# Between the two steps: the order of list sums, logits, moments and keys

## The chip, the cores and the metric

The kernel runs on one core of one Trainium2 chip. The metric is device time in microseconds (us), the median of several executions. A core has five engines with instruction queues of their own: TensorE (PE in the profile, its weight loads PEld), VectorE (DVE), ScalarE (ACT), GpSimd (POOL) and SyncE (SP, which here only issues DMAs). Line numbers (L819) are those of the kernel before.

## The reference

The input is a table of 3327 nodes with 256 features and a sparse weighted adjacency matrix. The table is normalised (layer norm, ReLU) and run through two steps. In each step a list part (`R @ Xf`, over each node's few neighbours) and an attention part (`A @ Xa`, over all nodes) are formed; in the attention, every row keeps only its largest probabilities until they make up 0.9 of the mass.

```python
R = S + jnp.eye(N)
R = R / R.sum(-1, keepdims=True)
for n in range(STEPS):                       # 2 steps
    q = Xa @ W1.T @ W2.T
    k = Xa @ W3.T
    probs = softmax(q @ k.T)
    A = probs * top_p_mask(probs, 0.9)
    A = A / A.sum(-1, keepdims=True)
    Xf = R @ Xf
    Xa = A @ Xa
    Z = Z + Xf @ U1[n].T + Xa @ U2[n].T
return x + layernorm(X + Z) * ln_g + ln_b
```

What matters for the change: keys `k` of step 1 come from `Xa` of step 0, for all nodes. A full row of step-1 logits can't be made before the last tile of step 0 has been summed and its keys are there.

## The kernel before

The nodes are cut into NT = 26 tiles of 128 rows (the last has 127). For each step a loop runs i from -1 to 27, and works on several tiles at once, each at another stage: `measured(i + 1)` guesses a threshold on ACT (passes over a whole row of 3328 elements, `ja`), `settle(i)` finds the exact one on DVE (`w`, `cand`, `bb`, `e`), the class `Sums` transposes the kept weights (`turn`, tiles `pt` and `eT`) and multiplies them with the node table (`sum`, tile `pa`), `spread` forms the list sums of a tile (`diffuse`, tile `pr`) and in step 0 writes the result to `vx` in DRAM, and `weights` makes a tile's logits in four chunks (`pl` on PE, then an exponential into `e` on ACT). In step 0, `first_end(t)` takes a summed tile, transposes it (`xa` to `xT`), multiplies it with the weights of both steps (`pz`: the second half goes to `xw`, the first to `sv` and to DRAM), and calls `prep`, which makes the tile's step-1 keys and queries (`pk` to `after` and `both`).

The order is written out by hand. One turn of the loop has seven slots; a string for each slot names generators by letters, and each letter advances its generator by one `yield`. `PLAN[0]` is the string list of step 0, `PLAN[1]` that of step 1, `OPEN` and `LAST` replace it in the first and last turns of step 1. The letters that matter: `s` list sums, `e` `first_end`, `w` the next logits chunk, `q` a tile's query projection, `m` and `n` `measured`, `d` and `c` `settle`, `g` gathers, `l` `laws` (the statistics of all tiles of step 1). A dependency from each instruction to the next of the same engine, added at the end of the kernel, keeps PE, ACT and DVE in the order of the text from the first turn on, and POOL from the start of step 1 on. SP's DMAs are not held to the text.

Names and lines around the border between the steps, in the order of the text:

- The last two turns of step 0 are i = 26 and i = 27 (NT and NT + 1). Both follow `PLAN[0]`. `spread(0, 24)` (L905, L1079, L1080) runs in slots 0 and 1 of turn 26, `spread(0, 25)` in slots 0 and 1 of turn 27.
- `begun` holds the `weights` generators of step-1 tiles 0, 1 and 2. Three of the four chunks of each are run in turns 24, 25 and 26; the fourth needs the keys of tile 25.
- At the end of turn 26 stand `moments(1, gsum)` (L504 to L510: DVE, PE, DVE) and three `project` calls (L522 on PE, L529 on ACT, L535 on DVE, L538 to L542 on POOL), which give tiles 0 to 2 the statistics that `measured` needs.
- In turn 27 `first_end(25)` makes `pz` (L918), has ACT copy it (L919, L921), and then makes the last keys (L482, L490, L491).
- Step 1 begins with the fourth chunk of tile 0 (`run(begun[0])`, L605, L607), then `prove(0)`, 12 or so small DVE operations (L771 to L788). Then comes turn -1 with `OPEN[-1]`: eight groups of `laws` (PE L554, DVE L557 to L560) on the letter `l`; `measured` of tile 0 on `m` (ACT L617 to L622, passes L630; DVE L681, L682; ACT L683 to L685; pass L630; DVE L695 on; ACT L698 to L701, L708); the fourth chunks of tiles 1 and 2 on two `w` in slot 2; five indirect gathers from `vx` (POOL L897) in slot 3, ahead of POOL's L686 to L688 of slot 4.
- Turn 0 of step 1 settles tile 0 (DVE L725, L730, ...) and measures tile 1. It has four letters `w`, which find nothing to do in the kernel before.

PSUM tiles rotate: `pt` (also used by `pk`, `pq` and others) has two buffers, `pl` two, `pr` (also `pz`) one, `pa` one.

Of the kernel before, what the change touches and what calls it, by code (L numbers as in the profile page):

```python
# [9 lines left out]
F32 = mybir.dt.float32  # L10
# [8 lines left out]
P = 128  # L19
N = 3327  # L20
D = 256
DA = 64
NT = (N + P - 1) // P
# [321 lines left out]
def guess_graph_layer(ctx, tc, x, adj, w1t, w2t, w3t, u1t, u2t, ln_g, ln_b, out, flag):  # L345
# [17 lines left out]
    rows_of = lambda t: min(P, N - t * P)  # L363
# [114 lines left out]
    def prep(xT, t):  # L478
        j, h = divmod(t, 2)
        pk = ps_t.tile([P, 4, P], F32, tag="pt", name="pk")  # L480
        for c in range(ND):
            PE.matmul(pk[:, 0, :], wk[:, c, h * DA : h * DA + P], xT[:, c, :], start=c == 0, stop=c == ND - 1)  # L482
        if t in COUNTED:
            for c in range(ND):
                PE.matmul(pk[:, 1, :DA], xT[:, c, :], wk[:, c, :DA], start=c == 0, stop=c == ND - 1)
        kp = (low, high)[h]
        kr = krs[:, t // 2 % 2, :]
        if t in COUNTED:
            S.copy(kr[:, :DA], pk[:, 1, :DA])
        S.copy(after[kp, j, :], pk[kp, 0, :])  # L490
        S.copy(query_of(t), pk[query_at(t), 0, :])  # L491
        if t not in COUNTED:
            return
        yield
        pg = ps_t.tile([P, 4, P], F32, tag="pt", name="pg")
        PE.matmul(pg[:DA, 0, : DA + 1], kr[:, :DA], kr, start=True, stop=True)
        gt = small.tile([DA, DA + 1], F32, tag="gt", name="gt", bufs=2)
        S.copy(gt, pg[:DA, 0, : DA + 1])
        G.tensor_tensor(gsum, gsum, gt, ALU.add)
# [292 lines left out]
    class Sums:  # L792
# [18 lines left out]
        def sum(self, g):  # L811

            t, k = divmod(g, PARTS)
            if k == 0:
                self.pa = ps_a.tile([P, 2 * D], F32, tag="pa", name="pa")[:, :D]
            eT = self.eT.pop(g)
            for c in range(4 * k, min(4 * k + 4, NT)):
                j = c % HALF * 2 + c // HALF
                PE.matmul(self.pa, eT[:, c - 4 * k, :], self.xa[:, j, :], start=c == 0, stop=c == NT - 1)  # L819
            if k < PARTS - 1:  # L820
                return None
            if self.step:
                return t, (self.pa, self.live.pop((self.step, t))["ra"])
            n = rows_of(t)
            dst = row.tile([P, D], F32, tag="xa", name="xa", bufs=2)
            if n < P:
                V.memset(dst, 0.0)
            S.activation(dst[:n], self.pa[:n], AF.Copy, scale=self.live.pop((self.step, t))["ra"][:n])
            return t, dst

# [82 lines left out]
    def first_end(t):  # L913
        aT = transposed(live.pop(("r", t)))
        yield
        pz = ps_r.tile([P, 2 * D], F32, tag="pr", name="pz")
        for c in range(ND):
            PE.matmul(pz, aT[:, c, :], u2[:, c].rearrange("p n d -> p (n d)"), start=c == 0, stop=c == ND - 1)  # L918
        S.copy(xw[:, t, :], pz[:, D:])  # L919
        sv = row.tile([P, D], F32, tag="sv", name="sv", bufs=2)  # L920
        S.copy(sv, pz[:, :D])  # L921
        G.tensor_tensor(sv, sv, x0[:, t, :], ALU.add)  # L922
        nc.sync.dma_start(sx[t], sv)
        yield
        yield from prep(aT, t)


    def finish(t, y, pa, ra):
# [135 lines left out]
    nc.sync.dma_start(bet, ln_b.to_broadcast([P, D]))  # L1064


    def spread(step, t):
        rr = rrs[:, t : t + 1]
        own = row.tile([P, D + 1], F32, tag="own", name="own", bufs=2)
        nc.sync.dma_start(*((own[:, :D], vx[:, t, :]) if step else (own, bx[:, t, :])))  # L1070
        s1 = row.tile([P, D], F32, tag="s1", name="s1", bufs=4)
        nc.sync.dma_start(s1, (sx if step else ax)[t])
        a, w = acs.pop(t), D + 1 - step
        pr = yield from diffuse(a, xgs.pop(t), own[:, :w], w)
        if step == 0:
            nc.sync.dma_start(cx[t], a.rearrange("p k r -> p (k r)"))
        yield
        if step == 0:
            V.reciprocal(rr, pr[:, D : D + 1])  # L1079
        V.scalar_tensor_tensor(s1, pr[:, :D], rr, s1, ALU.mult, ALU.add)  # L1080
        if step == 0:
            nc.sync.dma_start(vx[:, t, :], s1)
        else:
            live["f", t] = s1

    def refetch(t):
# [11 lines left out]

    LAST = {NT - 1: ("cfss", "cn", "nd", "sss", "fdddddsf", "f", ""), NT: ("c", "", "", "ff", "ff", "fv", "f"),
            NT + 1: ("fv", "f", "", "", "f", "f", "f")}  # L1100
    OPEN = {-1: ("llcmss", "lnms", "lwwnfd", "lcmdsssggggg", "fmgswqdf", "llmdf", "lmwfdm"),
            0: ("cmssggg", "nms", "wwnfd", "cmdsss", "fsmgwqdf", "mdf", "mwd"),
            1: ("cmss", "nms", "wwnfd", "cmdsssggggg", "fsmwqdf", "mgdf", "mwd")}
    OPEN[2] = OPEN[3] = OPEN[1]
# [7 lines left out]
    for step in range(2):  # L1112
        sums = Sums(step, live, xw if step else x0, AHEAD[step])

        for i in range(-1, NT + 2):
            if step == 0 and i == NT - 3:
                begun = [weights(1, t, live, False) for t in range(3)]
            if step == 1 and i == -1:
                ordered.append(len(trace))
            if step == 1 and i == -1:  # L1120
                run(begun[0])
                prove(0)
                for e in es[4:]:
                    G.memset(e[:, N:NP], 0.0)
            work.update(
                n=work["m"],
                c=work["d"],
                d=settle(step, i, live[step, i]) if valid(i) else none,
                m=measured(step, live[step, i + 1]) if valid(i + 1) else none,
                s=spread(step, i - 2 + 2 * step) if valid(i - 2 + 2 * step) else none,  # L1130
                w=later.pop((step, i + 2), none),
                e=first_end(i - 2) if step == 0 and valid(i - 2) else none,
                a=itertools.islice(lister, 9 if i else 3) if step == 0 else none,
                p=packed(i + 1) if step == 0 and i >= 0 and valid(i + 1) else none,
                g=fetching if step else gathered(i) if valid(i) else none,
                b=none, q=none, v=proof() if step and i == NT else work.get("v", none),
                l=laws(range(3, NT)) if step and i == -1 else work["l"] if step and i == 0 else none,
            )
            if i >= 0 and valid(i + 3):
                later[step, i + 3] = weights(step, i + 3, live)  # L1140
                work["q"] = itertools.islice(later[step, i + 3], 2 - step)
            if step == 0 and i >= NT - 2 and i < NT + 1:

                work["w"] = itertools.islice(begun[i - NT + 2], CUT - 1)
            if step == 0 and i >= NT - 3 and i < NT:
                work["q"] = itertools.islice(begun[i - NT + 3], 1)
            if i == -1:
                work["w"] = begun[1] if step == 0 else itertools.chain(begun[1], begun[2])
            if step == 0 and i == 0:
                work["w"] = begun[2]  # L1150
            if step == 0 and i < 1:
                work["b"] = itertools.islice(product, MADE if i else NT)
            for k in range(PARTS):
                g = PARTS * (i - 1) + k - LATE[step]
                summing = valid(g // PARTS)
                if step and valid((g + AHEAD[1]) // PARTS):
                    sums.turn(g + (k == 2), min(i, NT - 1))
                for c in "bb" + ({**OPEN, **LAST}.get(i, PLAN[1]) if step else PLAN[0])[k]:
                    next(work[c], None)
                if summing and not step:  # L1160
                    sums.turn(g, min(i, NT - 1))
                for n in BLOCKS[step].get(k, (0,)) if summing else ():
                    ended = sums.sum(g + n)
                    if ended and step == 0:
                        live["r", ended[0]] = ended[1]
                    elif ended:
                        work["f"] = finish(ended[0], live.pop(("f", ended[0])), *ended[1])
            if step == 1 and i == -1:
                run(work["m"])
            if step == 0 and i == -1:  # L1170
                G.memset(es[2][:, N:NP], 0.0)
            if step and i < 1:
                next(fetching)
            for c in ("lcnwqsepb" if i > -1 else "cnwqsepb") if step else "cmwqsepgb":
                run(work[c])
            if step == 0 and i == NT:
                moments(1, gsum)
                for t in range(3):
                    live[1, t]["ms"] = returned(project(1, t, queries=False))
    run(work["f"])  # L1180

    for engine, since in ((PE.engine, begin), (S.engine, begin), (V.engine, begin), (G.engine, ordered[0])):
# [47 lines left out]
```

## Time and profile before

| | |
|---|---|
| time, median of 3 runs | 1404.44 us (1404.25 to 1408.04) |
| profiled execution, its own time | 1405.77 us |
| its span, first to last instruction | 1404.0 us |
| granted TensorE clock, mean | 0.981 |
| busy share of the span: PE, DVE, ACT, POOL | 91%, 85%, 79%, 57% |
| step 0, last list sum of tile 25 ends on DVE (L1080) | 783.36 us |
| step 1, first full-row scan on DVE (L725), tiles 0, 1, 2 | 806.58, 828.51, 849.98 us |

The profile is of one execution. Its times count from the first instruction. The 1.77 us between its span and its own time lie before and behind the instructions. "Busy" is the time in which an engine executed something; for PE the ends of matmuls are modelled. A bracket behind an instruction gives the idle time of its engine before it and the instruction that ended the wait.

Busy time in 10 us stretches around the border between the steps (us of 10):

| us from start | PE | DVE | ACT | POOL | granted clock |
|---|---|---|---|---|---|
| 740 to 750 | 10.00 | 6.39 | 4.33 | 8.14 | 1.00 |
| 750 to 760 | 10.00 | 1.14 | 3.74 | 2.12 | 1.00 |
| 760 to 770 | 10.00 | 0.17 | 4.13 | 0.10 | 1.00 |
| 770 to 780 | 9.14 | 0.76 | 2.77 | 1.83 | 1.00 |
| 780 to 790 | 8.78 | 6.52 | 4.64 | 4.69 | 1.00 |
| 800 to 810 | 6.48 | 7.62 | 8.89 | 5.44 | 0.67 |
| 820 to 830 | 4.81 | 9.37 | 9.01 | 8.43 | 0.54 |
| 830 to 840 | 8.82 | 9.72 | 8.24 | 8.28 | 1.00 |
| 850 to 860 | 8.86 | 9.89 | 9.02 | 7.79 | 1.00 |

### The profile page before, as it was taken

How to read it: one execution, taken by the hardware profiler on the slowest of the kernel's cores; microseconds unless marked ns; L12 is line 12 of the kernel's file. 1: busy time of each engine (PE TensorE's matmuls, PEld its weight loads, DVE VectorE, ACT ScalarE, POOL GpSimd, SP SyncE). 2: the span in 40 equal slices, each digit the busy share in tenths (PEclk: the TensorE clock that was granted, in tenths of full speed). 3: DMA queues.
4: the chain of work that ended last, by engine and by line, in shares of the span. 5: the costliest groups of instructions: out<-in, count | busy, mean ns of one | idle time of the engine just before them, and what ended most of it. 6: DMA issues, size and time to landing. Idle time of an engine off the chain costs nothing.

```text
span 1404.0 us, 22095 instructions
## 1 busy us (share of the span) xinstructions
PE 1275.7 (91%) x6495; PEld 976.9 (70%) x6495; DVE 1195.0 (85%) x3673; ACT 1105.3 (79%) x2451; POOL 795.3 (57%) x1243
## 2 busy tenths in 40 slices
PE   6897999999999999999999759999999999999985
PEld 5545777777767777777777537777777777777764
DVE  6878898898988979989882489999998999999993
ACT  5467777878877778778773689999998999999941
POOL 6225766666657656666673475655655555565522
PEclk9999999999999999999999879999999999999998
DMA  8884453444444534534422121322312223132200
GB/s 279 269 269 122 118 145 109 128 138 117 128 125 115 143 107 122 146 111 125 126 78 83 51 72 45 90 77 60 91 56 80 67 70 88 50 89 73 63 20 22
DMA packets 91203, 149.77 MB, mean 107 GB/s; under 512 B 15266, under 2 KB 58657, under 8 KB 91073
## 3 DMA queue, kind: packets, MB, share of 16 engines
q1 hardware_dynamic: 73616, 105.37, 23.8%
q0 software_dynamic: 16640, 42.69, 12.3%
q8 instruction: 54, 0.88, 0.3%
q14 instruction: 77, 0.62, 0.1%
q10 hardware_dynamic: 816, 0.20, 0.1%
HBM read 120.93 MB, written 27.28 MB: 106 GB/s over the span
## 4 chain that ended last, share of the span: by engine, by line
PE 43%; DVE 40%; ACT 11%; issue 4%; DMA 1%; POOL 1%; SPq 0%; another core or an unknown queue 0%; DVEq 0%; ACTq 0%; POOLq 0%
PE pa L819 18%; DVE cand L730 8%; DVE w L725 7%; PE pt L805 6%; DVE e L759 5%; PE pr L905 4%; PE pl L597 4%; DVE cand L739 3%; ACT ja L630 3%; DVE bb L737 3%; PE pz L982 3%; PE pz L918 3%; DVE x L759 2%; ACT eT L807 2%; PE pk L1023 1%
## 5 line engine op out<-in xcount | busy, mean ns | idle before, releaser
L819 PE MATMUL pa<-xw,eT 128*128 128x256 f32 x1352 | 323.6, 384 | 27.4 <-DVE s L929 26.2
L630 ACT ACTIVATE ja<-e,g 128x3328 uint8<-128x3328 f32 x106 | 325.7, 3073 | 0.1
L819 PE MATMUL pa<-x,eT 128*128 128x256 f32 x1352 | 325.2, 382 | 0.0
L819 PEld LDWEIGHTS pa<-xw,eT 128*128 128x128 f32 x1352 | 250.7, 190 | 77.9 <-DVE s L929 31.6
L807 ACT COPY eT<-pt 128x512 f32<-128x512 f32 (+1 forms) x364 | 200.6, 559 | 119.8 <-PE pt L805 100.5
L819 PEld LDWEIGHTS pa<-x,eT 128*128 128x128 f32 x1352 | 244.8, 192 | 26.3
L730 DVE MAX8 cand<-w 128x8 f32<-128x168 f32 (+1 forms) x1040 | 251.4, 317 | 0.0
L805 PE MATMUL pt<-ident,e 128*128 128x128 f32 x1144 | 176.1, 276 | 18.2 <-DVE e L756 9.1
L897 POOL DMA_INDIRECT xg<-bx,index x130 | 156.6, 1205 | 45.2 <-issue 31.5
L805 PEld LDWEIGHTS pt<-ident,e 128*128 128x128 f32 x1144 | 140.9, 144 | 57.7 <-issue 29.2
L725 DVE SCALAR_TENSOR_TENSOR w<-e,g 128x3328 f32<-128x3328 f32 x44 | 162.1, 3684 | 0.7
L888 POOL DMA_INDIRECT ac<-in_adj,index x130 | 130.3, 1002 | 44.5 <-issue 29.6
L897 POOL DMA_INDIRECT xg<-vx,index x130 | 129.5, 996 | 38.6 <-issue 38.6
L759 DVE SCALAR_TENSOR_TENSOR e<-e,rec 128x3328 f32<-128x3328 f32 x40 | 147.5, 3688 | 0.6
L905 PE MATMUL pr<-xg,ac 128*128 128x257 f32 (+1 forms) x520 | 140.6, 395 | 6.8 <-DVE s L1080 6.8
L601 ACT ACTIVATE e<-pl 128x832 f32<-128x832 f32 x132 | 113.8, 867 | 17.9 <-PE pl L597 14.4
L905 PEld LDWEIGHTS pr<-xg,ac 128*128 128x128 f32 x520 | 94.0, 194 | 32.1 <-issue 14.2
L737 DVE MAX8 bb<-cand 128x8 f32<-128x160 f32 x286 | 92.6, 324 | 6.4
L597 PE MATMUL pl<-after,qT 64*128 64x416 f32 x416 | 95.5, 553 | 0.0
L597 PE MATMUL pl<-both,qT 64*128 64x416 f32 x416 | 90.4, 538 | 0.8 <-DVE both L1000 0.8
L673 POOL TENSOR_SCALAR g<-g,law 128x1 f32<-128x1 f32 x23 | 46.4, 2017 | 67.4 <-ACT g L672 67.4
L922 POOL TENSOR_TENSOR sv<-sv,x 128x256 f32<-128x256 f32 x26 | 19.8, 763 | 109.9 <-ACT sv L921 109.9
(255 smaller groups left out, 2153.5 us busy)
## 6 DMA issues: line engine op xcount, KB each, us to landing
at<-in_adj SPq DMA_DIRECT2D x102, 256.0 KB
cx<-ac SPq DMA_DIRECT2D x26, 384.0 KB
ac<-cx SPq DMA_DIRECT2D x26, 384.0 KB
wide<-in_adj SPq DMA_DIRECT2D x10, 832.0 KB
e<-in_adj SPq DMA_DIRECT2D x8, 832.0 KB
bx<-e SPq DMA_DIRECT2D x26, 128.5 KB
own<-bx SPq DMA_DIRECT2D x26, 128.5 KB
x<-in_x SPq DMA_DIRECT2D x13, 256.0 KB
```

The costliest lines, as they stand in the source:

```text
L597: PE.matmul(pl[:, a, :wd], qT[p, :], keys_of(step, a).rearrange("p a b -> p (a b)")[:, c : c + wd], start=True, stop=True)
L630: S.activation(ja, e, f, bias=guess, scale=sign, accum_out=total)
L725: V.scalar_tensor_tensor(w, e, col(16), e, ALU.is_lt, ALU.mult, accum_out=d2)
L730: V.max(cand[:, 8 * s : 8 * s + 8], w[:, s * SEG : min(NP, (s + 1) * SEG)])
L737: V.max(b8, cand)
L759: V.scalar_tensor_tensor(e, e, at(1), e, ALU.is_ge, ALU.mult, accum_out=ra)
L805: PE.transpose(pt[:, j, :], e[:, (j0 + j) * P : (j0 + j + 1) * P], ident)
L807: S.copy(eT[:, :w, :], pt[:, :w, :])
L819: PE.matmul(self.pa, eT[:, c - 4 * k, :], self.xa[:, j, :], start=c == 0, stop=c == NT - 1)
L888: G.indirect_dma_start(out=ac[:, k, :], out_offset=None, in_=rows, in_offset=bass.IndirectOffsetOnAxis(ap=index[:, t, k : k + 1], axis=0), ...
L897: G.indirect_dma_start(out=xg[:, k, :w], out_offset=None, in_=rows, in_offset=bass.IndirectOffsetOnAxis(ap=index[:, t, k : k + 1], axis=0))
L905: PE.matmul(pr[:, :w], ac[:, k, :], own if k == KT - 1 else xg[:, k, :w], start=k == 0, stop=k == KT - 1)
```

## The change

The order between the steps is written anew; no arithmetic is removed or added.

- The list sums of tiles 24 and 25 leave the first slots of turns 26 and 27 and run one behind the other in slots 2 to 5 of turn 27.
- `moments` goes to the last slot of turn 25, the three `project` calls to slots 0, 1 and 2 of turn 26 (`foreseen`).
- In turn 27 `first_end(25)` makes the last keys before `pz`; `pz` uses the buffer of `pa`, and DVE copies it instead of ACT.
- The fourth chunk of tile 0 goes into slot 2 of turn 27, that of tile 1 to slot 6 of turn -1 of step 1; the chunks of tile 2 all move from turn 26 and turn -1 to turn 0 of step 1, where the letters `w` stand in slots 2 (two), 4 and 6.
- The memset of the last summed tile's padding row goes ahead of the sum.

```diff
@@ Sums.sum
             if k == 0:
                 self.pa = ps_a.tile([P, 2 * D], F32, tag="pa", name="pa")[:, :D]
+                if not self.step:
+                    self.dst = row.tile([P, D], F32, tag="xa", name="xa", bufs=2)
+                    if rows_of(t) < P:
+                        V.memset(self.dst, 0.0)
...
-            n = rows_of(t)
-            dst = row.tile([P, D], F32, tag="xa", name="xa", bufs=2)
-            if n < P:
-                V.memset(dst, 0.0)
+            n, dst = rows_of(t), self.dst
@@ first_end
         yield
-        pz = ps_r.tile([P, 2 * D], F32, tag="pr", name="pz")
+        if t == NT - 1:
+            yield from prep(aT, t)
+            yield
+        pool, tag = (ps_a, "pa") if t == NT - 1 else (ps_r, "pr")
+        pz = pool.tile([P, 2 * D], F32, tag=tag, name="pz")
...
-        S.copy(xw[:, t, :], pz[:, D:])
+        copy = V.tensor_copy if t == NT - 1 else S.copy
+        copy(xw[:, t, :], pz[:, D:])
         sv = row.tile([P, D], F32, tag="sv", name="sv", bufs=2)
-        S.copy(sv, pz[:, :D])
+        copy(sv, pz[:, :D])
         G.tensor_tensor(sv, sv, x0[:, t, :], ALU.add)
         nc.sync.dma_start(sx[t], sv)
-        yield
-        yield from prep(aT, t)
+        if t < NT - 1:
+            yield
+            yield from prep(aT, t)
@@ new
+    def foreseen():
+        moments(1, gsum)
+        for t in range(3):
+            yield
+            early[t] = returned(project(1, t, queries=False))
+            if (1, t) in live:
+                live[1, t]["ms"] = early[t]
@@ plans
+    END = {NT - 1: ("mdsss", "mcdsss", "edwwp", "msd", "mpde", "gdwwq", "emgql"),
+           NT: ("l", "cl", "el", "", "e", "", "e"),
+           NT + 1: ("", "ee", "ssw", "ess", "sssss", "ssss", "")}
-    OPEN = {-1: ("llcmss", "lnms", "lwwnfd", "lcmdsssggggg", "fmgswqdf", "llmdf", "lmwfdm"),
+    OPEN = {-1: ("llcmss", "lnms", "lnfd", "lcmdsssggggg", "fmgsqdf", "llmdf", "lmwfdm"),
@@ the loop
-                s=spread(step, i - 2 + 2 * step) if valid(i - 2 + 2 * step) else none,
+                s=(itertools.chain(spread(0, NT - 2), spread(0, NT - 1)) if step == 0 and i == NT + 1 else
+                   spread(step, i - 2 + 2 * step) if valid(i - 2 + 2 * step) and (step or i < NT) else none),
...
-                l=laws(range(3, NT)) if step and i == -1 else work["l"] if step and i == 0 else none,
+                l=laws(range(3, NT)) if step and i == -1 else work["l"] if step and i == 0 else
+                  foreseen() if step == 0 and i == NT - 1 else work.get("l", none) if not step else none,
...
-            if step == 0 and i >= NT - 2 and i < NT + 1:
+            if step == 0 and i == NT + 1:
+                work["w"] = begun[0]
+            if step == 1 and i == 0:
+                work["w"] = begun[2]
+            if step == 0 and i >= NT - 2 and i < NT:
                 work["w"] = itertools.islice(begun[i - NT + 2], CUT - 1)
...
-                work["w"] = begun[1] if step == 0 else itertools.chain(begun[1], begun[2])
+                work["w"] = begun[1]
...
-                for c in "bb" + ({**OPEN, **LAST}.get(i, PLAN[1]) if step else PLAN[0])[k]:
+                for c in "bb" + ({**OPEN, **LAST}.get(i, PLAN[1]) if step else END.get(i, PLAN[0]))[k]:
...
-            if step == 0 and i == NT:
-                moments(1, gsum)
-                for t in range(3):
-                    live[1, t]["ms"] = returned(project(1, t, queries=False))
```

## The prediction

> **What bounds the kernel now.** I began with the chain of waits over the border (740 to 835 us); it is PE alone until the last keys, then ACT, then DVE:
>
> ```profile
> 761.63 1.60 PE pl L597 x8
> ...
> 776.76 0.38 PE pq L506 x2
> ...
> 778.96 1.50 PE pr L905 x6
> ...
> 782.87 0.49 DVE s L1080
> 783.37 0.14 issue
> 783.50 1.96 PE pz L918 x4
> 785.46 0.45 PE pk L482 x4
> ...
> 787.48 0.95 ACT e L605 x2
> ...
> 795.94 3.06 ACT ja L630 x2
> 799.00 0.03 issue
> 799.02 0.22 DVE g L681
> ```
>
> Columns: start, duration, engine, tile, line. Everything the change moves back (logits of tile 2, list sums, `pz`) stands here ahead of L605, the first ACT work that needs the last keys. Next, DVE's timeline, whose brackets give idle time, for what waits behind L605:
>
> ```profile
> 787.55 0.56 DVE L557 COPY wide<-pq 128x390 f32<-128x390 f32 x1 [0.59 <-PE pq L554]
> ...
> 799.02 0.21 DVE L681 TENSOR_SCALAR g<-oa,g 128x1 f32<-128x1 f32 x1 [4.11 <-ACT ja L630]
> ...
> 814.72 0.21 DVE L681 TENSOR_SCALAR g<-oa,g 128x1 f32<-128x1 f32 x1 [1.45 <-ACT ja L630]
> ```
>
> At 799.02 DVE, with five `laws` groups done, had waited only 4.11 us for ACT. That slack decides this case. Last, the chain from 832 us on:
>
> ```profile
> by line: DVE cand L730 19.3%; DVE w L725 16.6%; DVE e L759 10.7%; DVE cand L739 8.0%; DVE bb L737 7.5%; issue 5.6%; DVE x L759 5.3%; PE pa L819 2.4%; ACT ja L630 2.2%; DVE s L929 1.7%; DVE s L1080 1.7%; DVE dr L747 1.2%; DVE st L455 1.2%; D
> ```
>
> Step 1 is bound by DVE: L725 starts every 21.9 us (806.58, 828.51, 849.98). So what the change is worth is how much sooner DVE reaches L725 of tile 1, from where nothing differs.
>
> **The change part by part.**
>
> *Turn 25.* `moments` adds 0.38 us of PE (L506) between `pk` of tile 23 and the next transposes. The two `pt` buffers then force these to wait for ACT's copies of `pk` (until 753.74): they start at 753.8 instead of 753.01 (timeline). Loss about 0.65. DVE's four copies fall into its idle time.
>
> *To the last product of tile 25 (L819, ended 781.33).* From the stretch since 755.34 there go: list sums of tile 24, 2.6 (two pieces of 1.30 in the chain); three chunks of tile 2, 1.60 + 0.90 = 2.5; half the list sums of tile 25, 1.5; the block of `moments` and `project`, 776.76 to 778.96, 2.2, of which the six `project` matmuls stay (0.75; ACT and DVE follow in idle time). I add 0.25 for a `pt` wait after the transposes in slot 2. 2.6 + 2.5 + 1.5 + 2.2 - 0.75 - 0.25 - 0.65 = 7.2: the product ends at about 774.
>
> *To the last keys.* Next: ACT `xa` 0.5, transposes 0.4, `xT` 0.4, `pk` 0.65 with gaps 1.95 + 0.1; two list-sum matmul groups 0.87; the chunk 0.9. L605 starts at 777.8 instead of 787.48: **9.7 us sooner**. Beside the half of the sums, `pz` (1.96), DVE's 0.7 before it and the memset have left this path.
>
> *What is late next: DVE's queue.* The list sums now run behind that chunk, and PE's order is `pz` 1.72 (to 779.5), the rest of tile 24's sums 1.74 (781.2), L1079 and L1080 on DVE 0.8, which free the single `pr` buffer (782.1), tile 25's sums 2.6 (784.7), DVE's L1080 again: done at 785.5, where it was 783.36. Behind it in DVE's order stand `prove(0)`, 3.2 (783.27 to 786.5 in the timeline), and five `laws` groups, 7.4 (787.55 to 794.95): L681 at 796.1, L682 at 796.35, and ACT's L683, which needs it, at 796.65 instead of 799.52. ACT is through with both passes at 787.3 (9.7 for the keys, 1.95 for the two chunks that leave slot 2) and waits 9 us. **Of 9.7 + 1.95, 2.9 us remain.** DVE's 0.75 for copying `pz` (two 256-element copies; between the rows of L557, 390 elements 0.56, and 260 elements 0.43) lie before, in idle time.
>
> *Tile 0's scan.* The next pass and L695 follow ACT, 2.9 sooner. Slot 6 adds the chunk of tile 1 on ACT between L701 and L708, 0.98 (794.85 to 795.83 in the timeline, L605 with L607). L725 of tile 0: 806.58 - 2.9 + 0.98 = 804.7, **1.9 sooner**.
>
> *Turn 0.* Tile 2's four chunks, three of which cost nothing in ACT's idle time, now lie among ACT's passes. Two stand between tile 1's passes: 2 x 0.85 (spacing of neighbouring L601). The second pass ends 1.9 - 1.7 = 0.2 sooner, and DVE's L681, which waited for it at 814.72, gains 0.2, with its idle time grown from 1.45 to 3.3. The third chunk, 0.85, delays the third pass by 0.65 net; DVE had 0.4 of work over there (pass end 819.53, L695 at 819.95), so L695 is 0.3 later than before. The fourth, 0.98, delays L708, which DVE needs only at 828.2; ACT reaches it at 826.2. L725 of tile 1: **0.3 later**. In turn 1 ACT is 1.4 late and DVE 0.3; ACT waited 1.64 for DVE at 835.96, so that is absorbed.
>
> *Half clock.* In windows of 3.5 us, the clock of PE was 1.00 until 794.5, then 0.59 and 0.50, in the stretch where PE was busy 0.36 of 3.5 us. The Trainium skill ("TensorE: Matmul & The Clock Gate", Part 1 and "HAM oscillation") says that an idle window of some 3.4 us halves the clock, a rule against moving matmuls behind such a gap. By the row at full clock a chunk costs PE 0.90, by the row at 827.06 (2.73 for two) 1.37: tile 2's four cost 5.5 instead of 3.6. If PE set their pace, two would take ACT 2.7 instead of 1.7, and the sum would be 1.0 worse. PE has the first two done at about 806.4 and ACT asks at 809.6, so I take 1.7.
>
> *POOL and DMAs.* The gathers read `vx`, whose last write moves from 783.38 to about 785.7, behind SP's 384 KB load of `ac`. POOL reaches them at 781.5 and now waits, with L686 to L688 queued behind. In the trace of before they come at 791.98, long after the write, so it doesn't show how long a write takes to be seen. "DMA: Bandwidth & Descriptors" (Anatomy of one DMA) gives 2.0 us plus bytes at 436 GB/s: for 128 KB behind 384 KB an estimate of 3.2, so gathers from 789, and with five at 1.26 (791.98 to 798.1) POOL is free at 795.2. L686 is wanted at 797.8 and its result at 801. From below the wait costs nothing; from above, one us for each that the write is seen after about 793.5. I take nothing. The `sx` write of tile 25 is needed only at the end of step 1. The loads of `ac` for the next step wait on SP for the list sums, until 785; PE wants them at 799 or later.
>
> **Sum.** -2.9 + 0.98 + 1.7 + 0.5 (0.85 less the cover) = +0.3 us. Against the profiled execution's 1405.77 that is 1406.1; the runs' median is 1.3 below that execution, so 1404.44 + 0.3, **1404.8**.
>
> **The rivals.**
>
> 1. *DVE doesn't hold ACT*: then L605's 9.7 and the 1.95 arrive at tile 0's scan less 0.98 (10.7), and 8 are left after turn 0: 1396.5. For it: before, ACT always came last at L681. Against: 4.11 us of slack, and 2.1 of it gone by the later L1080. From 4.11 on, an earlier L605 is worth nothing.
> 2. *POOL's gathers wait for `vx`* (slower): L686 to L688 stand behind them, DVE's L695 takes L686's result. It decides from 793.5 on; it needs a write seen 12 us after issue to lose 4, which gives 1409. For it: the `ac` load ahead of the write and the strict order. Against: the estimate of 3.2 us.
> 3. *The last keys come no sooner*, because ACT's small copies stand in a row between PE's operations. Each us lost there is hidden by DVE's wait for up to 9 us; but if PE's list sums end later by as much, DVE follows. With 3 us lost to further buffer waits: 1407.8.
>
> **How the numbers follow.** About 0.3% (4.2 us) is what a measurement tells from no change. The forecast, DVE's queue giving back the gain, has 0.70; its own range is 1401.5 to 1408, since PE's stretch and DVE's chain are each known to some 1.5 us: same 0.63, faster 0.03, slower 0.04. Rival 1 has 0.11 (faster), rival 2 0.08 (slower 0.07), rival 3 0.11 (same 0.05, slower 0.06). Together faster 0.14, same 0.69, slower 0.17. From 1400 to 1409.5 the range leaves out rival 1 and the tail of rival 2.
>
> **What would show it.** Right: L605 of tile 0 near 778; a bracket of about 9 us before ACT's first L683, ended by L682; L1080 of tile 25 near 785.5 and `laws` without gaps; L725 of tile 0 near 804.7 and of tile 1 near 829; a period of 21.9 us after that. Wrong: L683 before 794 (rival 1), L686 or L695 waiting for POOL (rival 2), L605 after 781 (rival 3), or a wait that grows in turn 1, which would mean that ACT, not DVE, sets step 1's pace.

## The result and the profile after

The changed kernel takes 1406.99 us (median of 12 runs, 1402.12 to 1410.19) against 1404.64 for the kernel before (12 runs beside it): a ratio of 1.0008, 95% interval 0.9996 to 1.0019 (estimated over all these runs; the quotient of the two medians is 1.0017). No change can be told, as forecast (1404.8, within 0.3%).

The border looks quite different all the same. First the chain of waits of the changed kernel (start, duration, engine, tile, line; lines beyond 815 have shifted, L1095 is the old L1080, L923 the old L918):

```profile
772.74 0.48 ACT xa L829
...
774.88 0.87 PE pr L906 x4
775.75 0.90 PE pl L597 x4
776.65 1.91 PE pz L923 x4
778.56 1.75 PE pr L906 x8
780.31 0.81 issue
781.12 2.86 PE pr L906 x12
784.00 0.18 DVE rrs L1094
784.18 0.02 issue
784.21 0.48 DVE s L1095
784.69 0.09 DVE ok L771
...
787.75 0.49 DVE wide L557
...
794.78 0.14 DVE g L681
794.91 0.27 issue
795.19 0.40 ACT g L683
...
807.94 1.68 ACT e L601 x4
809.62 3.06 ACT ja L630 x2
```

Before, the chain went from PE through L605 to ACT's two passes. Now it stays on PE after tile 0's last chunk, runs through both list sums and `pz`, and then through DVE's proof (L771) and laws (L557) to L681. ACT's first two passes over tile 0 are no longer in it; the third, behind L683, still is. At 807.94 the first two chunks of tile 2 are on the chain, between two passes.

The timeline of the same kernel gives the waits in brackets:

```profile
776.72 0.86 ACT L605 ACTIVATE e<-pl 128x830 f32<-128x830 f32 x1 [1.26 <-PE pl L597]
...
795.19 0.39 ACT L683 ACTIVATE g<-g,one 128x1 f32<-128x1 f32 x1 [8.78 <-DVE g L681]
...
803.04 3.69 DVE L725 SCALAR_TENSOR_TENSOR w<-e,g 128x3328 f32<-128x3328 f32 x1
...
812.71 0.21 DVE L681 TENSOR_SCALAR g<-oa,g 128x1 f32<-128x1 f32 x1 [2.98 <-ACT ja L630]
...
827.07 3.69 DVE L725 SCALAR_TENSOR_TENSOR w<-e,g 128x3328 f32<-128x3328 f32 x1
```

ACT now waits 8.78 us for DVE where DVE had waited 4.11 for ACT, and DVE's idle time before tile 1's L681 has grown from 1.45 to 2.98.

Absolute times mislead here: this execution was 2.2 us ahead of the other before the border, in turns where both kernels are the same. So the marks in the table below, times of an event, are counted from one event of PE that lies ahead of all edits, the last query projection of step 0 (L520, at 750.25 before and 748.06 after). The first eight expectations, up to c8, count from DVE's scan L756 instead; in the first trace of the changed kernel L520 comes 6.76 later, so that their 53.9 is 47.1 here. The lines of a trace keep that trace's own times. Each ratio is to the kernel before, run beside it on the same chip; the experiments used four chips, on which the kernel before took 1405.20 (c1 to c4), 1365.42 (c5 to c8), 1391.53 (c9 to c11) and 1396.88 us (c12). Runs over 1.5% above the fastest of the same kernel on their chip are left out of the ratios.

| run | L605 tile 0 | ACT's wait at L683 | L683 | L725 tile 0 | L725 tile 1 | time, ratio to before |
|---|---|---|---|---|---|---|
| before | 37.2 | 0.53 | 49.3 | 56.3 | 78.3 | 1 |
| changed | 28.7 | 8.78 | 47.1 | 55.0 | 79.0 | 1.0008 (0.9996 to 1.0019) |
| changed, again | 28.7 | 8.89 | 47.2 | 55.1 | 79.1 | 1.0007 (0.9993 to 1.0020) |
| c2, proof early | 28.7 | 6.00 | 44.3 | 52.7 | 76.7 | 0.9985 (0.9976 to 0.9995) |
| c3, chunks in the wait | 28.6 | none | 51.7 | 58.7 | 80.6 | 1.0023 (1.0013 to 1.0032) |
| c4, before, proof early | 37.2 | 0.53 | 49.3 | 56.3 | 78.3 | 1.0004 (0.9990 to 1.0018) |
| c5, chunks ahead of laws | 28.7 | 1.47 | 47.3 | 54.4 | 76.3 | 0.9982 (0.9972 to 0.9993) |
| c6, c5 and c2 | 28.7 | 1.50 | 47.4 | 54.4 | 76.3 | 0.9987 (0.9979 to 0.9996) |
| c7, c6 and two laws | 28.7 | 1.58 | 47.4 | 54.7 | 76.6 | 0.9989 (0.9980 to 0.9997) |
| c8, products first | 30.4 | 7.22 | 47.3 | 55.1 | 79.2 | 1.0005 (0.9996 to 1.0014) |
| c9, c2 and interleaved | 28.7 | 1.63 | 45.7 | 52.7 | 74.7 | 0.9999 (0.9976 to 1.0022) |
| c12, c9 again | 28.6 | 1.64 | 45.7 | 52.7 | 74.6 | 0.9996 (0.9953 to 1.0039) |
| c10, c9 and two laws | 28.6 | 1.69 | 45.7 | 55.0 | 76.9 | 0.9974 (0.9948 to 1.0000) |
| c11, c10, gathers behind | 28.7 | 1.63 | 45.7 | 52.8 | 77.2 | 0.9998 (0.9974 to 1.0021) |

### The profile page after: what moved, and what is told of

It reads as the page before. It is cut to its first block, busy times and chain, and to the rows that moved or that the text cites. A ratio compares the mean times of both kernels' runs of the same rounds, so it can differ in the third digit from the quotient of the medians.

```text
span 1403.2 us, 22094 instructions
## 1 busy us (share of the span) xinstructions
PE 1281.2 (91%) x6495; PEld 979.2 (70%) x6495; DVE 1194.5 (85%) x3675; ACT 1104.7 (79%) x2449; POOL 794.5 (57%) x1243
## 4 chain that ended last, share of the span: by engine, by line
DVE 43%; PE 42%; ACT 9%; issue 4%; DMA 1%; POOL 0%; DVEq 0%; SPq 0%; ACTq 0%; POOLq 0%
PE pa L823 17%; DVE cand L730 9%; DVE w L725 7%; PE pt L805 6%; DVE e L759 5%; PE pr L906 4%; PE pl L597 4%; DVE cand L739 4%; DVE bb L737 3%; PE pz L989 3%; PE pz L923 3%; ACT ja L630 2%; DVE x L759 2%; ACT eT L807 2%; DVE fm L842 1%
## 5 line engine op out<-in xcount | busy, mean ns | idle before, releaser
L823 PEld LDWEIGHTS pa<-xw,eT 128*128 128x128 f32 x1352 | 251.2, 191 | 76.6 <-DVE s L936 29.9
L725 DVE SCALAR_TENSOR_TENSOR w<-e,g 128x3328 f32<-128x3328 f32 x44 | 162.1, 3684 | 0.7
L898 POOL DMA_INDIRECT xg<-vx,index x130 | 129.5, 996 | 47.3 <-issue 38.4
```

Of the source, the lines that this page charges most:

```text
L725: V.scalar_tensor_tensor(w, e, col(16), e, ALU.is_lt, ALU.mult, accum_out=d2)
L898: G.indirect_dma_start(out=xg[:, k, :w], out_offset=None, in_=rows, in_offset=bass.IndirectOffsetOnAxis(ap=index[:, t, k : k + 1], axis=0))
```

## The experiments

The theory: the last keys come 8 to 9 us sooner, but DVE holds ACT at L683, as its queue has the list sums, the proof and five groups of laws in front of L681; and tile 2's chunks, now between ACT's passes, use up what is left. The rival: ACT, fed by the last keys, still sets the pace.

**The changed kernel once more** (c1).

> The changed kernel once more, beside the three below. All marks in these runs are counted from the start of the second half of tile 25's kept-weights scan (L756, 2304 elements) in each trace, so that what a run gains or loses ahead of the border doesn't count. First profile: L605 of tile 0 at 35.4, ACT's first L683 at 53.9 after a wait of 8.8, L725 of tile 0 at 61.7, of tile 1 at 85.8 (before: 44.0, 56.0, 63.1, 85.0). Both theories: the same again within 0.5 us each; time against before +0.8 us, between -0.5 and +2.6.

All marks came back within 0.1 us.

**The proof out of DVE's way** (c2 in the changed kernel, c4 in the kernel before, there ahead of `moments`).

```diff
                 run(begun[0])
-                prove(0)
...
                 run(work[c])
+            if step == 0 and i == NT:
+                prove(0)
```

> The changed kernel with the proof of step 0 (some 12 DVE operations, 3.1 us) moved from ahead of step 1 to the end of turn 26, where DVE is idle and all its inputs are there. Theory (DVE's queue holds ACT): the first L683 comes 3.1 us sooner (50.8), its wait shrinks from 8.8 to 5.7, L725 of tile 1 3.1 sooner (82.7), the time is 3 us below the changed kernel. Rival (ACT, by the last keys and its own passes, sets the pace, and DVE is only beside it): L683 and the time stay within 0.5 us.

> The same move of the proof, in the kernel before (to the end of turn 26, ahead of the moments). Theory: there DVE has 4.1 us of slack at its first L681 and ACT comes last, so L683 stays at 56.0, DVE's wait at L681 grows from 4.1 to some 7, and the time stays that of before within 0.7 us. Rival (DVE's work at the border costs its length in any order): 3 us faster, as in the changed kernel.

L683 in c2, by the timeline:

```profile
796.63 0.39 ACT L683 ACTIVATE g<-g,one 128x1 f32<-128x1 f32 x1 [6.00 <-DVE g L682]
```

Of the move's 3 us, ACT's wait lost 2.8, L683 came 2.8 sooner and L725 of tile 1 2.3; the ratio fell from 1.0007 to 0.9985 (about 3 us). The missing 0.5 is POOL's: it was still behind with the gathers, and ACT's L708 now waited for it, as it had not in the changed kernel (DVE's L710 waited 1.53 for POOL as well):

```profile
804.34 0.29 ACT L708 ACTIVATE g<-g 128x1 f32<-128x1 f32 x1 [0.38 <-POOL g L706]
```

In the kernel before, c4, the same move did nothing:

```profile
787.59 0.56 DVE L557 COPY wide<-pq 128x390 f32<-128x390 f32 x1 [4.20 <-PE pq L554]
...
799.06 0.21 DVE L681 TENSOR_SCALAR g<-oa,g 128x1 f32<-128x1 f32 x1 [4.12 <-ACT ja L630]
```

DVE's freed time turned into a longer wait for the first laws matmul, 4.20 for 0.59, not into the longer wait at L681 that I expected; L681 itself still waited for ACT. The same 3 us of DVE are on the path after the change and off it before. That tells theory from rival.

**The last keys' own lead** (c8: `pz` of tile 25 ahead of its keys again).

```diff
-           NT + 1: ("", "ee", "ssw", "ess", "sssss", "ssss", "")}
+           NT + 1: ("", "eee", "ssw", "ss", "sssss", "ssss", "")}
@@ first_end: as before, but in pa's buffer and copied by DVE
-        if t == NT - 1:
-            yield from prep(aT, t)
-            yield
...
-        if t < NT - 1:
-            yield
-            yield from prep(aT, t)
+        yield
+        yield from prep(aT, t)
```

> The changed kernel with one part undone: the products of tile 25 (1.96 us of PE) ahead of its keys again, the rest as changed. Theory (ACT has 8.8 us to spare before L683): L605 of tile 0 about 1.9 later (37.3), ACT's wait at L683 1.9 shorter (6.9), L683 and L725 of tile 1 within 0.4 us of 53.9 and 85.8, time as the changed kernel within 0.7 us. Rival (the keys are on the path): 1.9 us slower.

```profile
755.07 0.39 ACT L683 ACTIVATE g<-g,one 128x1 f32<-128x1 f32 x1 [7.22 <-DVE g L682]
```

L605 came 1.7 later, the wait at L683 became 7.22, and nothing behind it moved by more than 0.2. "Last keys in front of products" buys nothing in this kernel.

**Tile 2's chunks** (c3: all five late chunks behind tile 0's second pass).

```diff
-    OPEN = {-1: ("llcmss", "lnms", "lnfd", "lcmdsssggggg", ...
+    OPEN = {-1: ("llcmss", "lnms", "lnfd", "lcmdssswwwwwggggg", ...
...
-            if step == 1 and i == 0:
-                work["w"] = begun[2]
...
-                work["w"] = begun[1]
+                work["w"] = begun[1] if step == 0 else itertools.chain(begun[1], begun[2])
```

> The changed kernel with the last logits chunk of tile 1 and all four of tile 2 put behind tile 0's second pass in turn -1, where ACT waits for DVE, instead of slot 6 of turn -1 and turn 0. Theory (these chunks are what takes the rest of the gain): ACT's first L683 stays at 53.9, its wait shrinks from 8.8 to about 4.4, L725 of tile 0 comes 1.0 sooner (60.7), DVE's L681 of tile 1 2.6 sooner, L725 of tile 1 3 sooner (82.8), the time is 3 us below the changed kernel. Rival (turn 0's chunks hide beside DVE's work, and DVE alone sets L725 of tile 1): no change at L725 of tile 1 beyond 1 us.

Slower instead. ACT's timeline in c3:

```profile
792.48 0.86 ACT L605 ACTIVATE e<-pl 128x830 f32<-128x830 f32 x1 [7.86 <-PE pl L597]
...
797.97 0.38 ACT L683 ACTIVATE g<-g,one 128x1 f32<-128x1 f32 x1
```

I had looked at ACT's order only. The chunks' matmuls stand behind the fifth group of laws on PE, and that group needs a `pt` buffer which DVE frees at its third. So ACT got its filling when its wait was over. PE's clock had a part too. PE had just waited 3.12 us for DVE ahead of the third group of laws, and its granted clock in 790.0 to 793.5 was 0.50: the first chunk's matmuls began at 790.41 and ACT got them at 792.48, where a chunk takes 0.90 at full clock (775.75 in the chain above). How much of the loss is the place and how much the clock, c3 alone can't tell. c5 puts the chunks ahead of the third group of laws in the text:

```diff
+    OPEN = {-1: ("llmmwwmwww", "l", "l", "lggggg", ...
```

> As the run with the chunks in ACT's wait, but with the five chunks ahead of the third and later groups of the laws in the text: three between tile 0's two passes, two behind the second. In that run PE made them only behind the fifth group, which waited for DVE to free a buffer, so ACT had them at 52.9 of the marks, when its wait was over. Theory (the chunks cost ACT time in turn 0, and PE's order alone spoiled the earlier run): L683 stays at 53.9 with a wait of about 4.4, L725 of tile 0 at 60.8, of tile 1 at 82.6 (3.2 sooner than in the changed kernel), time 3 us below the changed kernel (ratio to before about 0.9985). Rival (DVE alone sets tile 1): L725 of tile 1 within 1 us of 85.8.

```profile
747.95 0.86 ACT L605 ACTIVATE e<-pl 128x830 f32<-128x830 f32 x1 [2.68 <-PE pl L597]
...
757.43 0.39 ACT L683 ACTIVATE g<-g,one 128x1 f32<-128x1 f32 x1 [1.47 <-DVE g L682]
```

L683 stayed, its wait fell to 1.47, and L725 of tile 1 came 2.7 sooner than in the changed kernel: the ratio is 0.9982, its interval below 1 (c8, on the same chip, has 1.0005). PE made the chunks at clock 1.00 this time (747.0 to 754.0). The 1.47 is less than the 4.4 expected because L605 had waited 2.68 for PE, which had the list sums and two groups of laws to end first. **The chunks' place was the second loss.**

**Both** (c6, and c7 with two groups of laws at `"sswll"` in turn 27).

> The run before this one with the proof of step 0 moved to turn 26 as well. Theory: the two gains add, as ACT still waits some 1.6 for DVE: L683 at 51.1, L725 of tile 0 at 58.0, of tile 1 at 79.8, time about 6 us below the changed kernel, ratio to before 0.9963. Rival (steady turns of step 1 are bound elsewhere, and a sooner start is given back): L725 of tile 1 comes as sooner, but the time moves by less than 3 us.

> The run before this one, with the first two of the eight groups of laws in slot 2 of turn 27 behind tile 0's last chunk. They take 2.9 of DVE from behind the last list sum into idle time, and add about 1.5 of PE ahead of it. Theory: L683 1.2 sooner (49.9) and ACT's wait next to nothing, L725 of tile 1 at 78.6, time about 7 us below the changed kernel. Rival (PE's stretch is the tighter one): L683 later than 51.1, no gain over the run before.

The gains didn't add. DVE's timeline in c6 shows the third group of laws:

```profile
752.45 0.56 DVE L557 COPY wide<-pq 128x390 f32<-128x390 f32 x1 [3.12 <-PE pq L554]
```

DVE was free 3 us sooner and waited 3.12 for PE, which had the five chunks ahead of that group: it was at them from 746.38 to 751.59, of which 0.71 went to waiting until ACT had emptied one of two `pl` buffers. c7 freed DVE still more and gained nothing: DVE waited 5.07 for the third group there. c9 keeps the proof in turn 26 and puts two groups of laws between the chunks, all behind the second pass:

```diff
+    OPEN = {-1: ("llmmmwwllww", "", "", "lggggg", ...
```

> The proof in turn 26 and the five chunks in ACT's wait, but all behind tile 0's second pass, and with the third and fourth groups of the laws between the chunks in the text, so that PE isn't held by a chunk's buffer when DVE wants the third group (in the run with proof and chunks DVE waited 3.12 us for it at 42.7). Marks from here on count from PE's last query projection of step 0 (L520), as DVE's lead over PE in step 0 differs between chips: before, L683 49.3, L725 of tile 0 and 1 at 56.3 and 78.3; changed kernel 47.1, 55.0, 79.0; proof and chunks 47.4, 54.4, 76.3. Theory: third group at 40.2, L683 at 45.0 with a wait under 2.5, L725 of tile 1 at 74.0; time 4 us below before (ratio 0.997). Rival (ACT with its chunks is by now the bound): L683 stays near 47 and no wait is left in front of it.

> The kernel with the proof in turn 26 and the chunks and laws interleaved once more, as the times of its first comparison spread over 20 us on that chip, before and after alike. Theory: marks as there (L683 45.7, L725 of tile 0 and 1 at 52.7 and 74.7, against 56.3 and 78.3 before), so 3.6 us below before, a ratio of 0.9974, and the interval clear of 1. Rival (the sooner start of step 1 is given back in its steady turns): marks the same, but a ratio of 1 within 0.001.

In the traces this is the best version: L725 of tile 1 at 74.7 and 74.6, 3.6 us sooner than before, though DVE still waited 1.49 for its third group. From L520 to the end of the trace it took 651.3 and 651.1 us, against 653.8 before. The times don't confirm it: where these two ran, those of the kernel before alone spread over 22 and 27 us, both intervals hold 1, and that of c9 ends at 0.9976, short of the ratio of 0.997 that I expected.

**POOL's queue** (c10: c9 with two laws in turn 27; c11: the gathers moved behind).

```diff
+    OPEN = {-1: ("mmmwwllww", "", "", "lggggg", "fmgsqdf", "llmdf", "lmwfdm"),      # c10
+    OPEN = {-1: ("mmmwwllww", "", "", "l", "fmggsqdf", "llmdf", "lmggggwfdm"),      # c11
```

> The same with the first two groups of the laws in turn 27. Theory: DVE would be ready for L681 at 42.4, so L683 at 43.0 without a wait; but POOL's L686 comes behind five gathers that end at 48.2, so that DVE's L695 waits for POOL to about 48.7 instead of following ACT at 47.4: L725 of tile 0 at 51.4, of tile 1 at 73.3, ratio to before 0.9965. Rival (no wait for POOL): L695 at 47.4, L725 of tile 1 at 72.0.

> The run before this one with the gathers from the list sums' table moved behind the operations of POOL that tile 0's measurement needs (two in slot 4, four in slot 6 of turn -1). Theory: L695 follows ACT at 47.4, L725 of tile 0 at 50.1; but the list sums of tile 0 of step 1 come later, their L1095 stands in DVE's queue ahead of tile 1's L681, and from a gather end of 52 on that takes some back: L725 of tile 1 between 72.0 and 74.0, ratio to before 0.996. Rival (the gathers' place is free): L725 of tile 1 at 72.0.

L683 stayed at 45.7 in both, as PE held the third group of laws again, so that part of both expectations missed. In c10 POOL's gathers, the mechanism that the prediction had as its slower rival, cost more than in c2 (POOL's timeline, then a line of ACT's; the bracket at the gather names PE, but the work that the gather needs is the write of `vx`, issued at 777.77):

```profile
781.95 1.09 POOL L898 DMA_INDIRECT xg<-vx,index  x1 [10.24 <-PE pq L554]
...
788.09 0.28 POOL L686 TENSOR_SCALAR g<-g 128x1 f32<-128x1 f32 x1
...
791.40 0.31 POOL L706 TENSOR_SCALAR g<-g 128x1 f32<-128x1 f32 x1
```

```profile
791.75 0.29 ACT L708 ACTIVATE g<-g 128x1 f32<-128x1 f32 x1 [1.41 <-POOL g L706]
```

L695 waited 1.49 and L708 another 1.41 behind them; L725 of tile 0 lost 2.2 us to c9. In c11 that was gone (52.8), but the list sums of step 1 now came late:

```profile
802.98 0.48 DVE L1095 SCALAR_TENSOR_TENSOR s<-pr,rrs,s 128x256 f32<-128x256 f32 x1 [3.96 <-PE pr L906]
803.38 0.20 DVE L681 TENSOR_SCALAR g<-oa,g 128x1 f32<-128x1 f32 x1
```

L681 of tile 1 stands behind L1095 and had no wait of its own, and L725 of tile 1 came at 77.2, 2.5 later than in c9. The gathers' place is not free on either side. The ratio of c10, 0.9974, has an interval that ends at 1 and its marks are worse than c9's, so I draw nothing from it.

## Why the prediction was right

Changes of the changed kernel against before, on the common mark:

| step | predicted | measured |
|---|---|---|
| L605 of tile 0 | 9.7 sooner | 8.6 sooner |
| list sums end on DVE (L1080, now L1095) | 2.1 later | 3.5 later |
| ACT's wait at L683 | about 9 | 8.78 |
| L683 | 2.9 sooner | 2.1 sooner |
| L725 of tile 0 | 1.9 sooner | 1.35 sooner |
| L681 of tile 1, DVE's idle time before it | 0.2 sooner, 3.3 | 0.2 later, 2.98 |
| L725 of tile 1 | 0.3 later | 0.75 later |

- *The bound after the change.* Right, and shown by c2 against c4 and by c8: DVE's queue, with the late list sums at its head.
- *PE's stretch* was mis-sized by about 1 us. I gave six `project` matmuls 0.75 in one sum, where two of their three pairs took 0.42 each in the chain and the third lay beside a wait for ACT's copy of `xT`, and the transposes behind them took 0.59 to 0.66 instead of 0.44. The `pt` stall in turn 25 was there: transposes waited for `pk`'s copies and began 0.6 late, as forecast, and the product after them 0.85 late. Behind L605, `pz` took 1.91 for 1.72 and tile 25's sums 2.86 for 2.6, so that the list sums ended 1.4 later than forecast.
- *DVE's chain* from the list sums to L681 took 10.0 instead of 10.6 (784.69 to 794.69), which took back 0.6 of the 1.4. That the sum came so close is in part luck: these two errors were of opposite sign.
- *Turn 0* came as worked out: two chunks 1.68 between the passes, DVE's idle time absorbing part of them. The five late chunks cost 2.9 us from L683 to L725 of tile 1, where the sum had 0.98 + 1.7 + 0.5 = 3.2; c5, without them there, reached it 2.7 sooner. The idle time of 3.3 was a slip: 1.45 and the two chunks' 1.7 make 3.15.
- *POOL.* Right that it cost nothing: the first gather came at 789.92, L686 at 796.39, and L695 followed ACT at 799.59. The write of `vx` took longer to be seen than the estimate of 3.2 us, 4.2 from its issue at 785.71. The margin was about 1 us: POOL's L706 ended at 801.37 and ACT came to L708, which needs it, at 802.41. c2, with L683 2.8 sooner, used it up.
- *Half clock.* PE's clock fell sooner than before, in windows of 3.5 us to 0.63 from 788.5 and 0.50 from 792.0 to 799.0, right behind one with PE busy 0.38 us. It was not on the path here: DVE's groups of laws ran without a gap, and tile 2's first two chunks lay ready, as ACT read them back to back (1.68 for two).
- *Rival 1* fell by c2 and c8; *rival 2* appears where DVE is sooner and no longer hides it: 0.38 at L708 in c2, 0.27 in c7, most in c10. *Rival 3* was right in direction. L605's 1.1 was hidden by ACT's wait, but the list sums came 1.4 later too, and of that 0.8 reached L683.

From L725 of tile 1 to the end the two traces of the changed kernel took 0.6 and 1.2 us longer than the one before. The difference does not lie at the border. In all fourteen traces the time from tile 1's L725 to tile 21's is the same to within 0.6 us; most of the difference is in the last interval, from tile 24's L725 to tile 25's: 24.2 to 24.4 us before and in c4, c5 and c6, 25.0 to 25.6 in the other ten. There PE waits some 3.9 us for DVE, and the eight matmuls behind it took 2.4 to 2.7 us in the former and 3.2 to 3.8 in the latter:

```profile
1339.95 2.55 PE L819 MATMUL pa<-xw,eT 128*128 128x256 f32 x8 [3.96 <-DVE s L929]
...
1338.37 3.23 PE L823 MATMUL pa<-xw,eT 128*128 128x256 f32 x8 [3.94 <-DVE s L936]
```

The first line is of the kernel before, the second of the changed one. The granted clock in the first us of these matmuls was 1.00 before, 0.80 in the changed kernel and 0.50 in c9. Why it falls sooner in some traces, and whether the order at the border has a part in it, is not shown.

## What to carry to other kernels

An engine's work that is made ready sooner is worth only as much as the slack of the next engine at the point where they meet: read the bracket there (4.11 us here) before moving anything, and subtract what the move itself puts into that engine's queue. Work that is moved "behind" the critical thing should go into the wait that the move creates, and it has to be placed in every queue that it passes: in c3 ACT's order was right and PE's wrong, in c6 five chunks stood on PE ahead of the laws that DVE wanted. Small independent work (here a proof of 3 us) can go where its engine idles, ahead of the border; it pays only if that engine sets the pace behind it (2.3 us at L725 of tile 1 in c2, nothing in c4), and only up to the slack of the next engine, here POOL.

## What the runs showed of the hardware

A 128 KB write to DRAM, issued by SP right behind a 384 KB load, let the dependent gather start 4.1 to 4.4 us after the issue in four traces (4.21 in the changed kernel, 4.36 in c2, 4.13 in c9, 4.18 in c10). The prediction's estimate of 3.2 came from the fit in the Trainium skill ("DMA: Bandwidth & Descriptors", Anatomy of one DMA), which that section gives for DMAs of the GpSimd path; this write is SP's, so the estimate had been carried over to another path.

PE's granted clock fell right after a wait of some 3 us: in the changed kernel and in c3, PE waited 3.12 us for DVE ahead of the third group of laws, and the next two windows of 3.5 us show 0.63 and 0.50. In c5, where chunks stood in that place, it stayed at 1.00 until 754.0, some 3.5 us further on by the common mark.
